# Linear attention with memories beside a mixture of experts: a tile's local sums called with its memories, and fixed preferences in the planner of TensorE's order

## The chip, the cores and the metric

The kernel runs on one core of one Trainium2 chip, in one launch. The metric is the time of an execution in microseconds on the device. All numbers are 32-bit floats.

## The reference

The kernel computes one layer over 4096 tokens (4 sequences of 1024) with 256 channels: `x + attention(xn) + ffn(xn)`, where `xn` is the normalized `x`. Cut to what matters:

```
q, k, v = split(xn @ w_q.T), split(xn @ w_k.T), split(xn @ w_v.T)   # 16 heads of 16 channels
sq, sk = elu(q) + 1, elu(k) + 1

# memories: a sum of four ("coarse") and each of the four ("fine"), mixed by a learned gate
a_c, n_c = sq @ M, sq @ z                  # M, z: sums over the 4 memories and their norms
out_coarse = a_c / clip(n_c)
out_fine = sum over m of softmax(mean n_f)[m] * (sq @ memory[m]) / clip(sq @ norm[m])
gprob = sigmoid(relu(out_coarse @ eg_w1.T + eg_b1) @ eg_w2.T + eg_b2)
memory_output = gprob * out_fine + (1 - gprob) * out_coarse

# local: causal linear attention in chunks of 128 tokens, with a state S, z carried along
scores = (sq_chunk @ sk_chunk.T) * mask
num = scores @ v_chunk + sq_chunk @ S      # local sums, and those of the state
den = scores.sum(-1) + sq_chunk @ z
S, z = S + sk_chunk.T @ v_chunk, z + sk_chunk.sum()

output = (gate * memory_output + (1 - gate) * num / clip(den)) @ w_o.T

# ffn: 8 experts of 176, two per token by a softmax, and a shared one of 352
y = sum over the 2 experts of weight * ((silu(xn @ wg.T) * (xn @ wu.T)) @ wd.T) + shared(xn)
```

## The kernel before

The 4096 tokens are 32 tiles of 128, in 8 blocks of 512. The kernel first loads, normalizes and turns the input and computes values and the experts' logits; then it sorts tokens into 71 tiles of 128 expert slots while the first projections and the first block of the shared expert run. After that come 34 rounds, one for each tile of attention with its tail, with the 71 expert tiles spread over rounds 2 to 29 and the shared expert and the projections beside them. At the end the experts' sums are read back from memory and added.

Attention of a tile `n` consists of short functions, each of which issues one engine's work. TensorE's are called units here:

- `scores(n)` (L746): 16 matmuls of 16 or 32 rows into `quad`, a PSUM tile of four banks, all heads' scores.
- `mask(n, g)` (VectorE, L753), four of them: `quad` times the causal mask into the buffers `sT`, of which there are four, one for each `g`.
- `memory(n)` (L889): 8 matmuls with 32 rows of queries as weights and 170 columns, into `quad` again. It needs all four masks, which read `quad` before it is overwritten.
- `weigh(n)`, `fine(n, c)` (VectorE) and `gate_coarse(n)`, `sum_fine(n)` (GpSimd): the weighted coarse and fine outputs from `quad`. The next `scores` need both `fine`.
- `local(n)` (L772): 16 matmuls of 32 columns of values as weights, with `sT`, into a bank `pn`. It too needs the four masks, and the masks of tile `n + 1` need it, since they write `sT`.
- `local_copy(n)` (ScalarE, L784), then `back(n)` (L793, L799): the local sums turned back, with the state's product added in the same bank `pb`; then `weigh_local`, `base` and `update`, `state`, `add_state`.
- `turned(n)` (L950), `gate_hidden(n)` (L976), `gate_sum`, `gate_out`, `blend`: the gate between coarse and fine, and the transposition for the output product; `output(n)` (L1071, L1075).

An expert tile `j` is `expert_turn` (L1166, waits for the gathered rows `xg`, L1133), `expert_hidden` (L1183), `expert_out` (L1215), and a scatter-add `put` (L1229).

The order on each engine is not written by hand. A list `order` gives each function a place; `plan(order)` then simulates the engines with a table `cost`, the needs of each function (`needs`), four rotating PSUM banks, and calls the functions in the order found. Each of TensorE's functions gets a due time, which is the sum of the costs before it in `order`. At each step the planner looks at the next call of each function that has all its needs, finds when it could begin, and takes for TensorE the one with the earliest beginning, and among equals the smallest due time:

```
limit = window + min(place of the next call of each of TensorE's functions)
...
begin = max(ready, free[engine])
rank = (begin, due if engine == "PE" else ready)
if engine not in best or rank < best[engine][0]:
    best[engine] = rank, f
```

Calls whose place lies beyond `limit` aren't considered; `window` is 12 (in the same planned microseconds). In the list of a round, `memory` and `weigh` come first, then `gate_hidden` of the tile before and `fine`, then `local`, then `back` and `update`.

## Time and profile before

| | before |
|---|---|
| median of 3 runs | 651.66 us (651.62 to 651.92) |
| the profiled execution | 651.07 us |
| its span | 649.4 us |
| granted clock of TensorE | 0.998 of full speed |
| TensorE's matmuls busy | 627.6 us |
| VectorE, GpSimd, ScalarE busy | 429.5, 408.6, 278.5 us |

A float matmul shows as two records in the trace, so the 16 matmuls of `local` are 32 rows, and the 8 of `memory` 16. Records of matmuls overlap, since the engine is pipelined and their ends are modelled; the distance between the starts of two successive units tells what the first one takes. Groups are named by the tile that they write and those that they read: `quad<-mem,sqT` is `memory`, `quad<-sqT,skT` and `quad<-sqT,skO` are `scores`, `pn<-sT,va` is `local`, `pb` is `back`, `pu<-va,sk` is `update`, `phe` is `expert_hidden`, `pye` is `expert_out`, `pte` is `expert_turn`, `ph` is `gate_hidden`.

### The profile page before, as it was taken

Reading aid. Unit: us, or ns where it says so; the run is one execution under the profiler, and the core shown is the slowest. Engines: PE = TensorE matmul, PEld = TensorE weight load, DVE = VectorE, ACT = ScalarE, POOL = GpSimd, SP = SyncE. Lnnn points to the kernel's source line nnn. Section 1 sums busy time; section 2 is a strip of 40 time slices with the busy share of each in tenths; the row PEclk is TensorE's granted clock in tenths of the full one; section 3 lists DMA queues with packets and bytes.
Section 4 is the critical chain, followed back from the end, with each engine's and each line's share of the span. In section 5 each row is a group of like instructions: output and inputs, shape, how many; then the busy total and the mean of one; then the engine's idle time right before and its main releaser. Section 6 shows DMA issues by size and latency. Waiting matters only on the chain.

```text
span 649.4 us, 15187 instructions
## 1 busy us (share of the span) xinstructions
PE 627.6 (97%) x5510; PEld 487.9 (75%) x5510; DVE 429.5 (66%) x1205; ACT 278.5 (43%) x676; POOL 408.6 (63%) x456
## 2 busy tenths in 40 slices
PE   4999999989999999999999999999999999999996
PEld 3884467778888877777786777788888886778775
DVE  6837999966665566566656765666655656667751
ACT  3765455444444454334533444333445434344320
POOL 5310055677777876565665665677777498586876
PEclk9999999999999999999999999999999999999999
DMA  9779000156566753443443444346666675564278
GB/s 301 242 238 248 0 1 2 50 168 166 133 152 144 164 129 87 106 107 77 109 118 78 106 107 98 89 106 138 154 151 160 149 161 127 147 164 99 26 225 301
DMA packets 94379, 86.51 MB, mean 133 GB/s; under 512 B 12033, under 2 KB 91905, under 8 KB 94177
## 3 DMA queue, kind: packets, MB, share of 16 engines
q1 hardware_dynamic: 78976, 65.34, 34.5%
q0 software_dynamic: 13632, 18.62, 16.6%
q10 hardware_dynamic: 1696, 1.58, 0.7%
q8 instruction: 44, 0.72, 0.5%
q14 instruction: 31, 0.25, 0.1%
HBM read 67.56 MB, written 23.59 MB: 140 GB/s over the span
## 4 chain that ended last, share of the span: by engine, by line
PE 89%; DVE 6%; ACT 1%; DMA 1%; issue 1%; POOL 0%; DVEq 0%
PE phe L1183 14%; PE pye L1215 11%; PE po L1071 6%; PE psu L1030 6%; PE pg L1010 5%; PE quad L746 5%; PE pn L772 5%; PE pv L407 5%; PE po L1075 4%; PE quad L889 4%; PE pq L649 3%; PE pk L649 3%; PE pte L1166 3%; PE pb L793 2%; PE pb L799 2%; PE found L617 2%
## 5 line engine op out<-in xcount | busy, mean ns | idle before, releaser
L1229 POOL DMA_INDIRECT sums<-y,islot x71 | 112.6, 1585 | 56.5 <-ACT y L1224 16.1
L1183 PEld LDWEIGHTS phe<-turned,wgu 128*128 128x128 f32 (+1 forms) x852 | 102.2, 187 | 14.9 <-issue 12.9
L1183 PE MATMUL phe<-turned,wgu 128*128 128x128 f32 (+1 forms) x852 | 108.0, 276 | 0.0
L1133 POOL DMA_INDIRECT xg<-xns,islot x71 | 71.4, 1006 | 58.0 <-PE pte L1166 43.9
L753 DVE TENSOR_TENSOR sT<-quad,causal 128x512 f32<-128x512 f32 x128 | 79.4, 682 | 21.9 <-PE quad L746 9.5
L1215 PE MATMUL pye<-wdn,hidden 112*128 112x256 f32 (+1 forms) x284 | 77.9, 396 | 0.5
L1200 DVE SCALAR_TENSOR_TENSOR the<-the,phe 128x256 f32<-128x256 f32 x71 | 29.5, 415 | 43.3 <-ACT the L1195 30.0
L1215 PEld LDWEIGHTS pye<-wdn,hidden 112*128 112x128 f32 (+1 forms) x284 | 48.8, 190 | 11.4 <-issue 3.2
L936 POOL TENSOR_TENSOR fm<-fm 128x512 f32<-128x512 f32 x32 | 48.2, 1506 | 4.2 <-DVE fm L923 4.2
L1224 ACT ACTIVATE y<-pye,wslot 128x256 f32<-128x256 f32 x71 | 33.4, 471 | 38.9 <-PE pye L1215 36.2
L1195 ACT ACTIVATE the<-phe 128x256 f32<-128x256 f32 x71 | 27.1, 382 | 51.6 <-PE phe L1183 45.8
L608 POOL TENSOR_TENSOR held<-ones,two 128x213 f32<-128x213 f32 (+1 forms) x22 | 16.3, 748 | 49.5 <-DVE ones L581 49.5
L1071 PE MATMUL po<-wd,h 128*128 128x256 f32 (+1 forms) x192 | 47.0, 380 | 0.0
L1010 PE MATMUL pg<-xnT,wg 128*128 128x512 f32 (+1 forms) x96 | 45.7, 598 | 0.5 <-DVE th L1040 0.5
L1030 PE MATMUL psu<-xnT,wu 128*128 128x512 f32 (+1 forms) x96 | 45.9, 600 | 0.0
L923 DVE TENSOR_TENSOR fm<-quad,rw 128x512 f32<-128x512 f32 x64 | 41.0, 682 | 0.2
L1071 PEld LDWEIGHTS po<-wd,h 128*128 128x128 f32 (+1 forms) x192 | 35.5, 190 | 6.1 <-issue 1.6
L916 POOL TENSOR_TENSOR cg<-coarse,gates 128x256 f32<-128x256 f32 x32 | 30.9, 964 | 13.9 <-DVE coarse L904 11.6
L1173 ACT COPY turned<-pte 128x256 f32<-128x256 f32 x71 | 26.5, 373 | 27.6 <-PE pte L1166 25.6
L1002 POOL TENSOR_TENSOR o<-o,loc 128x256 f32<-128x256 f32 x32 | 29.7, 929 | 7.8 <-ACT o L996 5.8
L772 PE MATMUL pn<-sT,va 128*32 128x128 f32 x1024 | 34.6, 276 | 0.0
L827 POOL TENSOR_TENSOR loc<-loc,cg 128x256 f32<-128x256 f32 x32 | 26.5, 827 | 12.7 <-DVE loc L817 12.0
(200 smaller groups left out, 1329.8 us busy)
## 6 DMA issues: line engine op xcount, KB each, us to landing
wdn<-in_w_down_dram SPq DMA_DIRECT2D x71, 224.0 KB
wgu<-in_w_gate_dram SPq DMA_DIRECT2D x71, 176.0 KB
wgu<-ups SPq DMA_DIRECT2D x71, 176.0 KB
xns<-x SPq DMA_DIRECT2D x8, 512.0 KB
sums<-in_x_dram SPq DMA_DIRECT2D x8, 512.0 KB
x<-in_x_dram SPq DMA_DIRECT2D x7, 512.0 KB
part<-sums SPq DMA_DIRECT2D x12, 256.0 KB
out_dram<-acc SPq DMA_DIRECT2D x12, 256.0 KB
```

The lines of the kernel that those rows point to most:

```text
L649: nc.tensor.matmul(pq, w[:, k, c * P : (c + 1) * P], xnT[:, k, :], start=(k == 0), stop=(k == NC - 1),)
L753: nc.vector.tensor_mul(sT, quad[:, g, :].rearrange("p (c t) -> p c t", t=P), causal[:, None, :].to_broadcast([P, NC * 2, P]),)
L772: nc.tensor.matmul(pn[CW * r : CW * (r + 1), q, :], wide[:, i, first : first + CW], st["sT", h // 2][:, c * 2 + h % 2, :], start=True, sto ...
L923: nc.vector.tensor_mul(fm[:, c].rearrange("p g m (r k) -> p g (m r) k", k=HD), quad[:, :, c * KM + KX + KN : (c + 1) * KM].rearrange("p g ...
L936: nc.gpsimd.tensor_add(fm[:, :, 0:2, :], fm[:, :, 0:2, :], fm[:, :, 2:4, :])
L1010: nc.tensor.matmul(pg[:n, :], wg[:, k, f * P : f * P + n], xnT[:, k, :], start=(k == 0), stop=(k == NC - 1),)
L1030: nc.tensor.matmul(pu[:n, :], wu[:, k, f * P : f * P + n], xnT[:, k, :], start=(k == 0), stop=(k == NC - 1),)
L1071: nc.tensor.matmul(po[:, :H], st["h", blk, f][:k, tok], wd[:k, f, :], start=(f == 0), stop=False)
L1133: nc.gpsimd.indirect_dma_start(out=xg, out_offset=None, in_=xns, in_offset=bass.IndirectOffsetOnAxis(ap=islot[:, j : j + 1], axis=0),)
L1183: nc.tensor.matmul(ph[: cols.stop - cols.start, s, :], wgu[:, k].rearrange("p g f -> p (g f)")[:, cols], xgT[:, k, :], start=(k == 0), sto ...
L1215: nc.tensor.matmul(py[:, :H], hT[:n, f, :], wdn[:n, f, :], start=(f == 0), stop=(f == 1))
L1229: nc.gpsimd.indirect_dma_start(out=sums, out_offset=bass.IndirectOffsetOnAxis(ap=islot[:, j : j + 1], axis=0), in_=st.pop(("y", j)), in_of ...
```

## The change

`memory(n)` now calls the matmuls of `local` (renamed `local_sums`) right behind its own, so they are one unit for the planner: its cost is 1.73 where `memory` had 0.85 and `local` 1.05, its needs are those of `memory` (the same four masks), it takes the bank that `local` took, and `local_copy` follows it. The entry of `local` in a round's list is gone, and `memory` has the weight of both. In `weigh` and `gate_coarse` the coarse output is kept under a second name, which changes no instruction.

The planner gets a table `prefer`: a fixed amount for each of TensorE's kinds of units is added to the due time when units that could begin at the same moment are compared. `window` goes from 12 to 14.

```diff
-    def local(n):
+    def local_sums(n):
...
+    def memory(n):
+
+        blk, i, tok = at(n)
+        sqT = st["sqT", blk]
+        for c in range(NC):
+            for g in range(NG):
+                rows = slice(32 * g, 32 * (g + 1))
+                nc.tensor.matmul(
+                    quad[:, g, c * KM : (c + 1) * KM], sqT[rows, c, tok], mem[rows, c, :],
+                    start=True, stop=True,
+                )
+        local_sums(n)
...
-        u += unit(560, memory, n) + unit(64, weigh, n)
+        u += unit(1120, memory, n) + unit(64, weigh, n)
 
         u += unit(256, gate_hidden, n - 1) + unit(64, fine, n, 0)
-        u += unit(560, local, n) + unit(64, fine, n, 1)
+        u += unit(64, fine, n, 1)
...
-            gate_hidden: [gate_sum], local: [local_copy], back: [weigh_local, base],
+            gate_hidden: [gate_sum], memory: [local_copy], back: [weigh_local, base],
...
-            scores: ("PE", 1.10), memory: ("PE", 0.85), local: ("PE", 1.05), back: ("PE", 0.92),
+            scores: ("PE", 1.10), memory: ("PE", 1.73), back: ("PE", 0.92),
...
-                mask: lambda: [(scores, n), (local, n - 1)],
+                mask: lambda: [(scores, n), (memory, n - 1)],
...
-                local: lambda: [(mask, n, g) for g in range(NG)],
-                local_copy: lambda: [(local, n), (back, n - 1)],
+                local_copy: lambda: [(memory, n), (back, n - 1)],
...
+        prefer = {
+            add_slots: -1.2, shared_gate: 1.4, scores: 4.0, shared_up: 4.2, keys_back: -1.1,
+            memory: -1.8, back: 2.9, update: 1.5, turned: -0.1, gate_hidden: -0.2, output: 3.6,
+            expert_turn: 1.7, expert_hidden: 1.9, expert_out: 0.5, project: -2.3,
+            batch_weights: 2.9,
+        }
         done, called = {}, {}
-        window = 12.0
+        window = 14.0
...
-                rank = (begin, due if engine == "PE" else ready)
+                rank = (begin, due + prefer.get(f, 0.0) if engine == "PE" else ready)
```

More of the change, by code (lines that the diff above doesn't have):

```diff
@@ L880, in add_state @@
         nc.gpsimd.tensor_add(new, new, old)
-    def memory(n):
-        blk, i, tok = at(n)
-        sqT = st["sqT", blk]
-        for c in range(NC):
-            for g in range(NG):
-                rows = slice(32 * g, 32 * (g + 1))
-                nc.tensor.matmul(
-                    quad[:, g, c * KM : (c + 1) * KM], sqT[rows, c, tok], mem[rows, c, :],
-                    start=True, stop=True,
-                )
     def weigh(n):
@@ L908, in weigh @@
             )
-        st["coarse", n] = coarse
+        st["coarse", n] = st["coarse to gate", n] = coarse
         st["rw", n] = rw
@@ L913, in gate_coarse @@
     def gate_coarse(n):
-        coarse = st["coarse", n]
+        coarse = st.pop(("coarse to gate", n))
         cg = tmp.tile([P, H], FP, tag="cg", name=f"cg_{n}", bufs=1)
```

## The prediction

> **What bounds the kernel now.** I read the page from the top, then the waits of TensorE, then TensorE's timeline unit by unit, because the page alone cannot say what a "busy" TensorE is busy with.

> ```profile
> span 649.4 us, 15187 instructions
> PE 627.6 (97%) x5510; PEld 487.9 (75%) x5510; DVE 429.5 (66%) x1205; ACT 278.5 (43%) x676; POOL 408.6 (63%) x456
> ...
> PE   4999999989999999999999999999999999999996
> ...
> DVE  6837999966665566566656765666655656667751
> ...
> PEclk9999999999999999999999999999999999999999
> ...
> PE 89%; DVE 6%; ACT 1%; DMA 1%; issue 1%; POOL 0%; DVEq 0%
> ```

> TensorE is busy in 97% of the span at full clock, and 89% of the chain that ended last is its own. Only slices 5 to 8 of the row DVE (65 to 115 us, where the expert lists are sorted and turned into slots) show another full engine. From there on the time is the length of TensorE's queue: what its units cost in their order, plus what it waits. The waits are short:

> ```profile
> PE pt L385 <- ACT x L367: 8.7, 2, 7.6
> PE pb L793 <- ACT nT L784: 2.4, 2, 1.2
> PE pte L1166 <- DMA xg<-xns,islot: 2.2, 2, 1.4
> PE pte L1166 <- issue: 1.1, 1, 1.1
> ```

> The first is the load of the input, which no edit touches. The second is two places where back (L793) stood waiting for local_copy (L784). The third is the first two gathers of expert rows.

> The timeline of TensorE shows what the busy share hides. A unit's price is the distance from its first start to the next unit's first start:

> ```profile
> 594.66 1.49 PE L1183 MATMUL phe<-turned,wgu 128*128 128x128 f32 x12
> 596.08 0.86 PE L889 MATMUL quad<-mem,sqT 32*128 32x170 f32 x16
> 596.88 1.13 PE L1215 MATMUL pye<-wdn,hidden 112*128 112x256 f32 x4
> 597.85 0.55 PE L976 MATMUL ph<-w,oc 128*128 128x64 f32 x4
> 598.24 1.55 PE L1183 MATMUL phe<-turned,wgu 128*128 128x128 f32 x12
> 599.71 1.08 PE L772 MATMUL pn<-sT,va 128*32 128x128 f32 x32
> 600.73 1.13 PE L1215 MATMUL pye<-wdn,hidden 112*128 112x256 f32 x4
> ...
> 608.53 0.86 PE L889 MATMUL quad<-mem,sqT 32*128 32x170 f32 x16
> 609.33 1.08 PE L772 MATMUL pn<-sT,va 128*32 128x128 f32 x32
> 610.34 0.73 PE L860 MATMUL pu<-va,sk 128*128 128x136 f32 x4
> ```

> The twelve records of phe last 1.42 us ahead of memory (594.66 to 596.08) and 1.47 ahead of local (598.24 to 599.71). Between two units of whole 128 x 128 weights the same twelve take 1.33 (the median of 44 units). So entering a unit of small weights costs 0.09 us, and into local up to 0.15. Leaving one costs too: pye behind memory takes 0.97 (596.88 to 597.85) where 0.87 is its price elsewhere. The last three lines are one of two places where this order already has local directly behind memory: memory still takes 0.80 and local 1.01, their prices everywhere. The step between them costs nothing, though one is 32 x 128 and the other 128 x 32.

> **The change part by part.**

> *Local behind memory.* It removes no instruction: the changed order has the same 623 units on TensorE with the same matmuls. It removes neighbours. Before, 30 of 32 tiles have other units between memory and local. Each pays four switches: into memory, out of it, into local, out of it. As one unit it pays the first and the last. Going through the order of before:
> - Entries into local that go, by the unit in front: 12 behind expert_out, 6 behind gate_hidden, 4 behind expert_hidden, 8 behind others. At 0.09 to 0.15, and 0.12 in the mean, 30 x 0.12 = 3.7 us.
> - Exits from memory that go: 15 into expert_out at 0.10, 6 into the short expert_turn at 0.055, 9 into others at 0.10: 2.8 us.

> Together 6.5 us. Scores keeps its own switches, which both orders have 32 times. Two or three tiles lie where VectorE is full, and there TensorE would only wait longer, so I count 28 of 30: **-5.9 us**.

> [...]

> *The wait for local_copy.* Before, back stands one expert_hidden behind local: 1.43 to 1.46 us of TensorE's work in half of the tiles. The copy alone is short, but ScalarE runs in order:

> ```profile
> 533.56 0.59 ACT L784 COPY nT<-pn 128x512 f32<-128x512 f32 x1 [3.23 <-PE pte L1166]
> ```

> ScalarE sat 3.23 us at an instruction ahead of this copy, waiting for expert rows to be turned, and back waited for both. In the changed order the median distance from local to back is 5.95 us and only two tiles are under 2. The row of 2.4 us goes. In the first rounds expert_turn 1 also moves behind back, which puts 0.9 us of work over its wait of 0.75 (what the row of 2.2 us has besides the first gather's 1.44). **-3.15 us**. The wait of 1.44 stays: the distance from the last slots to expert_turn 0 is the same in both orders. So does that of 1.1.

> *What the earlier call does to VectorE.* Masks of tile n+1 write the four buffers that local of tile n reads. In 6 tiles of before, local stands behind the next scores, and the masks show it:

> ```profile
> 205.87 2.48 DVE L753 TENSOR_TENSOR sT<-quad,causal 128x512 f32<-128x512 f32 x4 [2.10 <-PE pn L772]
> ```

> In the changed order local is at least 4.6 us ahead of the next scores, so this wait goes. It cost TensorE nothing before, as memory stood far behind. Weigh waits for memory's last matmul and not for local's: no cost. If it did wait 1.0 us more, the shortest way from memory to the next scores has 5.6 us, and weigh and both fines end 3.1 to 5.7 us behind memory, so nearly all of it would stay covered.

> *Preferred kinds and the wider window.* They trade distances. From the changed order, priced with the units above, against how long each chain took in the trace of before:
> - Scores to memory (four masks between): the median distance falls from 6.25 to 4.55 us, with 13 tiles at 2.99 to 3.92. The masks end 2.62 us behind the scores at best and 3.47 in the median, which includes the wait for local just shown. At 2.62 no tile waits; at 3.47 five do, for 1.45 us in all. I take the middle, 0.7.
> - Gate_hidden to turned (gate_sum, gate_out, blend on GpSimd): the median falls from 9.4 to 6.0, with seven tiles at 3.8 to 5.0. The chain took 2.99 at best and 5.05 in the median, with slack. At the median these seven would wait 4.3 us, at the best 0. I take 0.6, near the low end, since GpSimd's order is laid out anew for the nearer use.
> - Expert_hidden to expert_out: five at 2.45 and one at 1.76, against a median of 1.81: 0.1. At the ninth decile of 2.62 it is 1.7.
> - Turned to output and turned to gate_hidden grow (2.9 to 5.2, 6.6 to 9.5): nothing, and no gain, as TensorE did not wait there.

> Together **+1.4 us**, between 0 and 7.5. At the end, the last scatter on GpSimd moves forward, ahead of the gate of tile 30, so the parts are read back no later. The 12 totals (14.2 us) start right behind base of tile 31 and still end about with the last output; no cost. If they ended last, it would be by under 1 us. DMA traffic is the same.

> **Sum.** -5.9 - 3.15 + 1.4 = -7.65. The profiled span of 649.4 becomes 641.75. Its run took 651.07, so 1.67 lies around the span; the median of the runs shown, 651.66, is 0.6 above it. 641.75 + 1.67 + 0.6 = **644.0 us**.

> **The rivals.**

> [...]

> *Slower: the masks become TensorE's wait.* Memory, with local now behind it, stands nearer to its scores. If VectorE is behind its queue when the scores end (weigh_local and the silu of an expert stand just ahead of the masks), memory waits, and everything in TensorE's queue waits with it. Priced over the 32 distances: masks that end 4.25 us behind the scores in every tile cost 9.0 us, which eats both gains, and that is the point from which it decides. At 4.63 (the ninth decile before) they cost 15.1 us: 651.7 - 9.05 + 15.1 = 657.7. For it: VectorE at 66%, half of the tiles at or under 4.55. Against it: the long chains of before are mainly those that waited for local, and at the median chain the bill is 1.45.

> [...]

> **How the numbers follow.** The trace's own price of a switch with the short stalls: 0.65. The drain that stays: 0.22. Small waits that eat it, from no change to a little slower: 0.07. Masks that bind: 0.06. Two runs of this kernel can be told apart from about 0.2%, or 1.3 us. Faster by more takes the first two: 0.87. Of the third, 0.04 is within 0.2% and the rest is slower: 0.04 and 0.09. The range runs from 640.5 (no new waits, all 30 tiles, and something of the 1.44) to 649.5 (the drain that stays, with half of the small waits).

> **What would show it.** In the changed profile, phe ahead of memory should still take 1.42, memory 0.79 and local 1.01 with no gap between; phe, pye and the others should stand at their plain prices wherever local used to follow. The row of pb waiting for nT should be gone. [...] If masks bind, a row of quad waiting for sT on VectorE appears with several us. I am wrong if TensorE's busy time is not about 6 us below 627.6, or if its waits grow by more than they lose.

## The result: 3.2% slower, with the saved switches in it

The changed kernel takes 672.54 us (four runs, 670.84 to 673.82), that of before 651.64: a ratio of 1.0322, 95% interval 1.0295 to 1.0348. The profiled execution took 673.15 us, its span is 671.4. The forecast was 644.0.

The page after, in the lines that answer to those shown of before:

```profile
span 671.4 us, 15218 instructions
PE 632.0 (94%) x5510; PEld 494.9 (74%) x5510; DVE 437.6 (65%) x1205; ACT 280.2 (42%) x676; POOL 409.3 (61%) x456
...
PE   4999999999999889999998999999998999998996
...
PEclk9999999979999979999999999999999899998998
...
PE 74%; DVE 10%; POOL 10%; DMA 2%; ACT 2%; issue 2%; POOLq 0%; ACTq 0%
```

TensorE's share of the last chain fell from 89% to 74%, and GpSimd, which had none, now has 10%. The row PEclk has dips where before had full clock up to the last slice: the granted clock is 0.979 in the mean, where before had 0.998. TensorE's waits (total, times, longest):

```profile
PE pt L951 <- POOL o L1003: 9.4, 10, 2.2
...
PE pt L951 <- DVE hidden L1206: 3.7, 1, 3.7
PE pk L851 <- ACT y L1225: 3.4, 1, 3.4
PE pte L1167 <- DMA xg<-xns,islot: 2.4, 1, 2.4
PE pte L1167 <- issue: 2.1, 1, 2.1
```

The row of pb waiting for nT is gone, as foretold. In its place stands turned (`pt`) waiting for blend on GpSimd, ten times, and two single waits over 3 us.

TensorE's busy time, where about 6 us less was to be seen, is 4.4 us more (632.0 against 627.6): matmuls at half clock are busy too (from 138.40 to 141.80 us, at a granted 0.50, TensorE is busy all of the 3.40 us), so this sign can be read only in a run without them, further down.

The switches are gone too. All 32 tiles have memory directly in front of local, and there are 64 entries into units of small weights, where there were 94. The median distance from an expert_out to the next unit fell from 0.97 to 0.87 us, its price without a switch. TensorE's timeline at the first expert tiles:

```profile
131.00 0.86 PE L788 MATMUL quad<-mem,sqT 32*128 32x170 f32 x16
131.79 1.08 PE L772 MATMUL pn<-sT,va 128*32 128x128 f32 x32
132.80 0.66 PE L977 MATMUL ph<-w,oc 128*128 128x64 f32 x4
135.83 0.66 PE L1167 MATMUL pte<-ident,xg 128*128 128x128 f32 x2 [2.37 <-DMA xg<-xns,islot]
...
139.38 2.67 PE L1184 MATMUL phe<-turned,wgu 128*128 128x128 f32 x12
141.88 0.38 PE L1167 MATMUL pte<-ident,xg 128*128 128x128 f32 x2
```

Memory takes 0.79 us and local 1.01, with nothing between: over all 32 tiles 0.791 to 0.794 and 1.010 to 1.012. But phe, at 139.38, takes 2.50 us (to 141.88) for what costs 1.33 elsewhere. That is half clock (0.50 granted from 135.0 to 141.8), behind a wait of 2.37.

To see where the 22 us of span come from, I priced both orders of TensorE with the same plain prices and switches, and took the rest, unit by unit, as wait or half clock (units whose neighbours both are in the records). A wait is here all that lies above the price of the unit in front, a little more than the idle time in the profile's list (15.0 for turned, where the list has 9.4 and 3.7):

| us | before | after |
|---|---|---|
| the order at plain prices with its switches | 611.7 | 604.9 |
| above the price, in all | 16.4 | 44.0 |
| of it, ahead of 66 us | 4.1 | 4.1 |
| waits of turned | 0.3 | 15.0 |
| waits of expert_turn | 3.6 | 6.0 |
| waits of keys_back | 0.5 | 3.8 |
| waits of back | 3.2 | 0.3 |
| units at half clock, by its stretches in the middle | - | 9.1 |

The order got 6.8 us cheaper. The rest got 27.6 dearer, two thirds of it as waits and a third as half clock behind four waits of 2.23 to 3.69 us.

### The profile page after: what moved, and what is told of

The parts are those of the page before. It is cut to its first block, busy times and chain, and to the rows that moved or that the text cites. A ratio compares the mean times of both kernels' runs of the same rounds, so it can differ in the third digit from the quotient of the medians.

```text
span 671.4 us, 15218 instructions
## 1 busy us (share of the span) xinstructions
PE 632.0 (94%) x5510; PEld 494.9 (74%) x5510; DVE 437.6 (65%) x1205; ACT 280.2 (42%) x676; POOL 409.3 (61%) x456
## 3 DMA queue, kind: packets, MB, share of 16 engines
q0 software_dynamic: 13632, 18.62, 16.4%
## 4 chain that ended last, share of the span: by engine, by line
PE 74%; DVE 10%; POOL 10%; DMA 2%; ACT 2%; issue 2%; POOLq 0%; ACTq 0%
PE phe L1184 11%; PE pye L1216 7%; PE psu L1031 5%; PE quad L746 5%; PE po L1072 5%; PE pv L407 5%; PE pg L1011 4%; PE pn L772 4%; PE quad L788 4%; PE pq L649 3%; PE po L1076 3%; PE pk L649 3%; PE pt L951 2%; PE found L617 2%; POOL sums L1230 2%; PE pte L1167 2%
## 5 line engine op out<-in xcount | busy, mean ns | idle before, releaser
L1230 POOL DMA_INDIRECT sums<-y,islot x71 | 113.1, 1593 | 68.8 <-DMA sums<-y,islot 11.8
L1184 PE MATMUL phe<-turned,wgu 128*128 128x128 f32 (+1 forms) x852 | 113.4, 285 | 0.2 <-ACT sk L860 0.2
L1184 PEld LDWEIGHTS phe<-turned,wgu 128*128 128x128 f32 (+1 forms) x852 | 105.3, 194 | 6.7 <-issue 4.7
L753 DVE TENSOR_TENSOR sT<-quad,causal 128x512 f32<-128x512 f32 x128 | 79.4, 682 | 19.3 <-PE quad L746 16.7
L1216 PE MATMUL pye<-wdn,hidden 112*128 112x256 f32 (+1 forms) x284 | 75.3, 387 | 0.0
L1216 PEld LDWEIGHTS pye<-wdn,hidden 112*128 112x128 f32 (+1 forms) x284 | 50.3, 194 | 9.1 <-issue 3.9
L937 POOL TENSOR_TENSOR fm<-fm 128x512 f32<-128x512 f32 x32 | 46.8, 1462 | 6.7 <-DVE fm L924 6.7
L917 POOL TENSOR_TENSOR cg<-coarse,gates 128x256 f32<-128x256 f32 x32 | 25.6, 801 | 39.4 <-DVE coarse L905 39.1
L797 ACT COPY nT<-pn 128x512 f32<-128x512 f32 x32 | 18.7, 585 | 43.5 <-PE pn L772 43.5
L840 POOL TENSOR_TENSOR loc<-loc,cg 128x256 f32<-128x256 f32 x32 | 29.7, 930 | 10.8 <-DVE loc L830 10.7
L1003 POOL TENSOR_TENSOR o<-o,loc 128x256 f32<-128x256 f32 x32 | 31.1, 971 | 6.2 <-ACT o L997 5.0
```

The lines of the kernel that those rows point to most:

```text
L753: nc.vector.tensor_mul(sT, quad[:, g, :].rearrange("p (c t) -> p c t", t=P), causal[:, None, :].to_broadcast([P, NC * 2, P]),)
L937: nc.gpsimd.tensor_add(fm[:, :, 0:2, :], fm[:, :, 0:2, :], fm[:, :, 2:4, :])
L1184: nc.tensor.matmul(ph[: cols.stop - cols.start, s, :], wgu[:, k].rearrange("p g f -> p (g f)")[:, cols], xgT[:, k, :], start=(k == 0), sto ...
L1216: nc.tensor.matmul(py[:, :H], hT[:n, f, :], wdn[:n, f, :], start=(f == 0), stop=(f == 1))
L1230: nc.gpsimd.indirect_dma_start(out=sums, out_offset=bass.IndirectOffsetOnAxis(ap=islot[:, j : j + 1], axis=0), in_=st.pop(("y", j)), in_of ...
```

## The experiments

Each kernel's ratio is against before on its own chip and in the same rounds. "Charged" means that the planner counts something; "in the same order" means that only what a call issues differs.

**The merge alone, and the preferences alone.** The kernel after with `window` at 12 calls everything in the same order, so the window counts for nothing. The merge alone has no `prefer`:

```diff
-                rank = (begin, due + prefer.get(f, 0.0) if engine == "PE" else ready)
+                rank = (begin, due if engine == "PE" else ready)
```

> The merge without the table of preferences (the window is 12; with 14 the planner's order is the same). Theory: the switches saved (64 entries into small-weight units instead of 94, 6.6 us by the prices of the trace of before) were real, and the lost time came with the preferences, which cut the distances to blend and to the banks. Then this kernel has TensorE's waits of before or fewer, no half-clock stretches in the middle, and 643 to 648 us. Rival: the merge itself ties units together and makes the waits; then 660 to 675 us.

Measured: 663.17 us, ratio 1.0192 (1.0143 to 1.0242). The theory failed. The merge without any preference already makes three fifths of the whole loss. It has the cheap order (605.1, 64 entries) and pays for it with waits, and with three stretches of half clock in the middle, 13.7 us in all (the changed kernel has four, 23.9 us; at 2.50 us for a phe of 1.33, a little under half of such a stretch is lost at most):

```profile
PE pt L951 <- POOL o L1003: 4.5, 3, 2.3
PE pte L1167 <- DMA xg<-xns,islot: 2.6, 1, 2.6
PE pte L1167 <- DVE loc L830: 2.2, 1, 2.2
PE po L1072 <- DVE skT L673: 2.1, 1, 2.1
```

The preferences alone put `prefer` and the window of 14 into the kernel before.

> The table of preferences and the window of 14 on the kernel before, with memory and local separate units (local has no preference). Theory (preferences make the waits): TensorE waits 10 us or more beyond before, for blend and for banks, with half-clock stretches: 660 to 672 us. Rival (only the merged unit with preferences does harm): 648 to 655 us, as 3 entries fewer are worth under 1 us.

Measured: 662.37 us, ratio 1.0186 (1.015 to 1.0221), as the theory had it. TensorE waited for blend in six places, and two stretches of 3.4 us ran at half clock:

```profile
PE pt L950 <- POOL o L1002: 8.9, 6, 2.5
```

So each half of the change makes waits on its own, and together they come to somewhat less than their sum (1.9% and 1.9%, and 3.2% for both).

**Whose fault the waits are: the same order with a cause left out.** Three of the longest waits stand behind batch_weights. These are VectorE, GpSimd and TensorE there (start, duration; the wait in front in brackets):

```profile
231.53 2.52 DVE L711 TENSOR_TENSOR rel<-rel,top 128x64 f32<-128x64 f32 x1
...
232.16 1.81 POOL L937 TENSOR_TENSOR fm<-fm 128x512 f32<-128x512 f32 x1
...
235.51 0.41 DVE L1201 SCALAR_TENSOR_TENSOR the<-the,phe 128x256 f32<-128x256 f32 x1
235.95 0.29 DVE L1203 SCALAR_TENSOR_TENSOR hidden<-the,phe 112x128 f32<-112x128 f32 x1
236.25 0.29 DVE L1206 SCALAR_TENSOR_TENSOR hidden<-the,phe 64x128 f32<-64x128 f32 x1
...
236.69 0.66 PE L951 MATMUL pt<-ident,o 128*128 128x128 f32 x2 [3.69 <-DVE hidden L1206]
```

Turned waits for the last instruction of an expert's silu. It doesn't use its result: it needs the PSUM bank that this instruction frees, and silu stood behind the softmax in VectorE's queue. The planner counts batch_weights as one TensorE unit of 3.50 us, and nothing on VectorE. It does so in the order of before too. But the softmax itself grew: from its first VectorE instruction to its last it took 6.5 us here and 6.1 in the sequence at 515 us, where those of before took 2.6 to 3.0. The excess lies in a few instructions beside GpSimd's; the longest here, the product L711 with 2.52 us, ends at 234.05, just behind GpSimd's fm (233.97). In the next kernel the last three sequences leave the softmax out:

```diff
+        if b:
+            st["w5", b] = st["w5", 0]
+            return
         top = small.tile([P, NC, HC], FP, tag="top", name=f"top_{b}", bufs=1)
```

> The changed kernel in the same order on every engine, but the softmax over memories is done for the first of four sequences alone and its weights used for all (leaves out 10 VectorE and 1 ScalarE instructions for each of three sequences; the matmul of batch_weights and one copy stay). Theory: three of the longest waits (3.9, 3.5 and 2.3 us, at 233, 516 and 355 us) follow these blocks, because VectorE and so the release of PSUM banks is late by them, and two of them set off stretches at half clock (10.2 and 3.4 us, 6.8 us lost). They go: 655 to 660 us. Rival: these waits have another cause and stay: 668 to 673 us.

Measured: 657.19 us, ratio 1.0098 (1.0073 to 1.0123): as expected. The three waits and both stretches of half clock behind them are gone, and the waits of turned for blend stay:

```profile
PE pt L954 <- POOL o L1006: 13.1, 11, 3.0
```

The two other stretches are gone in this execution as well, though the first gather still holds TensorE 2.1 us, and there is a new one at 528.6, behind the wait of 3.0. So the gain of 15 us is mainly the softmax's, and in part a matter of where the half clock fell.

The waits of turned for blend are GpSimd's queue. Here is one of them, in GpSimd's rows and TensorE's:

```profile
606.34 1.59 POOL L1230 DMA_INDIRECT sums<-y,islot  x1 [1.16 <-DMA sums<-y,islot]
...
607.38 1.30 POOL L1003 TENSOR_TENSOR o<-o,loc 128x256 f32<-128x256 f32 x1
608.06 1.34 POOL L893 TENSOR_TENSOR state<-state,state 128x272 f32<-128x272 f32 x1
...
608.74 0.44 PE L951 MATMUL pt<-ident,o 128*128 128x128 f32 x2 [2.23 <-POOL o L1003]
...
609.23 2.58 PE L1184 MATMUL phe<-turned,wgu 128*128 128x128 f32 x12
```

Blend (L1003) stands behind a put that first waits 1.16 us for the put before it to land and then takes 1.59, to 607.93. GpSimd's records overlap, as TensorE's do: blend's begins before the put's ends, and ends at 608.68, 0.75 us behind it. That is blend's usual 0.73; its 1.30 are no slower addition. Then turned starts, and the phe behind it runs at half clock. In the next kernel put issues nothing:

```diff
     def put(j):
-        nc.gpsimd.indirect_dma_start(...)
+        st.pop(("y", j))
```

> The changed kernel in the same order, with the scatter-add of the experts' rows left out on GpSimd (71 instructions; the output lacks the experts). Theory: the waits of turned for blend (9.4 us in ten places, one followed by a half-clock stretch at 609 us) come from blend standing behind a put in GpSimd's queue, which itself waits for the expert's output or for the put before to land. They go: 656 to 662 us, and the page shows no row of pt waiting for o on GpSimd. Rival: blend is late through ScalarE's or VectorE's part of its chain: within 3 us of the changed kernel.

Measured: 649.61 us, ratio 0.9997 (0.9982 to 1.0011). Turned's waits fell from 15.0 to 1.3 us, none for blend on GpSimd. From the start of gate_hidden to the end of blend the median fell from 5.53 to 3.70 us. The gain, 23 us, is larger than expected, since the two long waits behind the softmax are shorter as well (keys_back 1.3 us where it had 3.5, turned 1.3 where it had 3.9), and half clock costs 4.0 instead of 9.1 us (three stretches of 3.4 us). The softmax took 3.9 us in these two places instead of 6.5 and 6.1, so the two causes touch each other.

Both left out:

> The changed kernel in the same order, with both left out: the scatter-add of the experts' rows on GpSimd, and the softmax over memories of the last three sequences. Theory: the two causes account for nearly all of the new waits, so what is left is the saved switches: no row of pt waiting for o, none of pk or pte waiting for ScalarE, at most the half-clock stretch at the first gather, and 639 to 644 us (about 8 under the run without put, which still had 6 us of waits behind the softmax and 3 us of half clock after them). Rival: waits move to other places once these are gone: 647 us or more.

Measured: 642.65 us, ratio 0.9866 (0.9837 to 0.9895), as expected. Its waits:

```profile
PE pt L385 <- ACT x L367: 8.9, 2, 7.7
PE pte L1170 <- DMA xg<-xns,islot: 1.8, 1, 1.8
PE found L617 <- ACT held L598: 1.5, 2, 0.9
PE quad L791 <- DVE sT L756: 0.5, 1, 0.5
```

This is the forecast's time in the changed order, without half clock in the middle. TensorE's busy time is 619.4 us, 8.2 below before, and it is done at 633.0 us instead of 644.0. Leaving the two out takes away the whole loss, and more. They aren't separate sums: left out one by one they give 15 and 23 us, together 30. And before itself was not run with the two left out, so what it would gain, and how near the forecast this comes by chance, stays open. It is no version of the kernel: the output lacks the experts and uses one sequence's weights for all.

**Can it be mended with everything computed?** The softmax as a call of its own for the planner:

```diff
-            update: ("PE", 0.48), ..., batch_weights: ("PE", 3.50),
+            update: ("PE", 0.48), ..., batch_weights: ("PE", 0.36), batch_softmax: ("DVE", 2.9),
```

> The changed kernel with the softmax of batch_weights made a call of its own for the planner (VectorE, 2.9 us, after a TensorE unit of 0.36; before it was one TensorE unit of 3.50), and weigh made to need it. All is computed. Theory: the planner then knows that VectorE is taken and leaves the waits behind batch_weights out, as leaving out the softmax did (657 us): 655 to 663 us. Rival: the lateness comes from GpSimd and VectorE contending, which no charge mends: 668 to 674 us.

Measured: 658.65 us, ratio 1.0114 (1.0082 to 1.0146): as expected. Charging the work brought nearly as much as leaving it out, though the planner's order changes with it. The softmaxes still took 3.8 to 4.8 us beside GpSimd's work, so the rival's cause may be there too, but a charge did mend most of the loss. In the profiled execution (655.16 us, the fastest of four) no half clock is left in the middle.

Then I asked the planner for more distance, in general: longer delays from each engine's end to its consumers and a dearer put, with preferences and without.

```diff
-        lag = {"PE": 0.22, "ACT": 0.06, "DVE": 0.06, "POOL": 0.06, "SP": 4.0}
+        lag = {"PE": 0.22, "ACT": 0.40, "DVE": 0.40, "POOL": 1.50, "SP": 4.0}
```

> The changed kernel with the softmax charged as its own call, a put counted as 2.2 us and 3.5 to land, and the planner's delay from an engine's end to its consumers raised (GpSimd 0.06 to 1.5, VectorE and ScalarE 0.06 to 0.4 us). The order then keeps gate_hidden to turned at 8.0 us in the median instead of 6.0, with the same 64 entries. Theory (switches saved, waits avoidable): most waits of turned go, no half clock in the middle: 642 to 650 us, faster than before. Rival (the merged order cannot have cover for all): 653 us or more.

> The merge without preferences, with the softmax charged, the put counted as above, and wider delays (GpSimd 3.0, VectorE and ScalarE 0.8 us). Gate_hidden to turned becomes 8.0 us in the median (6.7 with the merge alone), one at 3.5. Theory: 643 to 652 us, against 663 for the merge alone. Rival: 655 us or more.

Measured: 666.39 us, ratio 1.0216 (1.0189 to 1.0244), and 665.02, ratio 1.0209 (1.0179 to 1.0238). Both missed. In the first, turned's waits fell to 6.1 us, but others came (expert_turn 4.8, expert_hidden 2.9, output 2.4), and the end moved to another chain. The last expert_out began at 608.3 us and the last put only at 635.0. So the experts' sums were read back late, the totals on GpSimd ended at 659.7, and TensorE, done at 652.9, was 13 us ahead of the end. Before, its last put began at 617.8 and it was 5.4 ahead. A delay that the planner believes in also moves the puts back.

A put that stands back for whatever can begin within 1.5 us, again with the softmax charged, and with a gather's landing counted as 3.6 us instead of 2.0, so this is more than one change:

```diff
+        late_by = {put: 1.5}
...
-                rank = (begin, due + prefer.get(f, 0.0) if engine == "PE" else ready)
+                rank = (begin + late_by.get(f, 0.0), due + prefer.get(f, 0.0) ...)
```

> The changed kernel with the softmax charged as its own call, a gather counted as 3.6 us to land, and one rule more for GpSimd's queue: a put stands back for anything that can begin within 1.5 us of it in the plan. Theory (blend late behind a waiting put): turned waits 3 us or less for o, 647 to 654 us, against 658.7 with the softmax charged alone. Rival (the planner uses the earlier blend to pull turned forward again, and the waits stay): 656 to 662 us.

Measured: 702.87 us, ratio 1.0714 (1.066 to 1.0769), the worst of all. Turned's waits were 4.8 us, but the puts fell behind: the last expert_out began at 634.7 us, the last put at 669.4. Expert outputs waited in their three buffers, and TensorE waited for ScalarE, which writes them and frees their banks:

```profile
PE po L1077 <- DVE acc L1089: 6.4, 1, 6.4
PE pye L1221 <- ACT y L1230: 5.2, 3, 3.6
PE phe L1189 <- ACT y L1230: 4.3, 3, 2.5
PE pb L811 <- DVE hidden L1211: 2.9, 4, 1.7
PE pb L811 <- ACT y L1230: 2.8, 1, 2.8
```

**The order of before, with local moved and nothing else.** The planner works with before's costs and its own place for local; memory issues local's matmuls:

```diff
     def local(n):
+        pass
...
+        local_sums(n)        # at the end of memory(n)
```

> The order of before, planned with its own costs and no preferences; only the 16 matmuls of local are called right behind memory's, where the planner had them some units later. All 590 other units of TensorE stand in the same order as before (and so the cover that before's plan gave to every chain, less the 0.2 us a tile of saved switches). Theory (the switches are worth 6.5 us where the cover stays; what was lost is the planner's repacking around a bigger unit): 64 entries, no half clock in the middle, 643 to 647 us. Rival A (holding the bank of local's sums longer makes other units wait for a bank): 650 to 656 us. Rival B (the merge can't be had without the waits): over 656 us.

Measured: 662.88 us, ratio 1.0109 (1.0062 to 1.0156). Before took 655.84 us in these rounds. The theory failed again. By its size this is rival B's case (over 656 us), while rival A, with 650 to 656, names a good part of the waits:

```profile
PE pb L795 <- ACT nT L786: 4.8, 8, 1.0
PE ph L979 <- DVE sqT L669: 2.1, 4, 0.5
PE ph L979 <- DVE skT L673: 2.1, 4, 0.5
PE pte L1169 <- DVE ph L990: 2.1, 1, 2.1
PE pye L1218 <- ACT oc L968: 1.8, 4, 0.5
```

Gate_hidden (`ph`) has no use for sqT or skT, nor expert_out (`pye`) for oc. They wait for the banks that these instructions free. As I read it, local's sums now hold a bank for some units longer, while local_copy keeps its place in ScalarE's queue, and with four banks in rotation the next units find none. Back's waits for local_copy grew as well, from two to eight. And the one long wait, 2.1 us of the first expert_turn, was followed by 6.8 us at half clock.

**GpSimd out of the chain to turned.** One VectorE instruction in place of ScalarE's product and GpSimd's addition, in the order of the kernel with the softmax charged:

```diff
-        nc.scalar.activation(o, st.pop(("diff", n)), AF.Copy, scale=prob)
-        nc.gpsimd.tensor_add(o, o, st.pop(("base", n)))
+        nc.vector.scalar_tensor_tensor(
+            o, st.pop(("diff", n)), st.pop(("prob", n)), st.pop(("base", n)), ALU.mult, ALU.add
+        )
```

> The changed kernel with the softmax charged as its own call (658.7 us), in the same order of calls, but blend is one VectorE instruction (diff times prob plus base, about 0.42 us) in place of a ScalarE product (0.51) and a GpSimd addition (0.73 to 1.3). No put stands ahead of it any more. Theory: the waits of turned (7 us in eight places for o on GpSimd) go: 644 to 652 us, with everything computed. Rival (VectorE, in order too, makes turned wait as long): 656 us or more.

Measured: 654.06 us, ratio 1.0019 (0.9997 to 1.0042). The row of turned waiting for GpSimd is gone, and as with the softmax charged there is no half clock in the middle of the profiled execution (649.58 us, the fastest of ten); turned's waits fell from 9.8 to 3.5 us, now for VectorE's queue and for banks. It is the time of before, not less: the forecast of 644 to 652 was missed by 2 us. TensorE's busy time shows the saved switches here, with everything computed:

```profile
PE 621.4 (96%) x5510; PEld 485.7 (75%) x5510; DVE 454.1 (70%) x1237; ACT 265.6 (41%) x644; POOL 388.6 (60%) x424
```

That is 6.2 us below before's 627.6, and with the softmax charged alone it is 5.1 below. The time doesn't follow: the idle time between TensorE's records adds up to 20.7 us, and to 16.4 before.

> The kernel before in its own order, with the same blend on VectorE. Theory: before has 9 us of cover for this chain in the median and no wait of turned, so nothing is gained: within 2 us of before, or slower by VectorE's additional 13 us of work spread over the span. Rival (the move helps any order): 3 us or more faster than before.

Measured: 649.81 us, ratio 0.9985 (0.9956 to 1.0014): no difference that can be told, as expected. The median of before was 652.99 in these rounds, but its runs lie between 648.82 and 654.81.

> As j2, but the planner is told (blend 0.45 on VectorE, gate_out 0.50 on ScalarE) and packs turned nearer again: gate_hidden to turned 5.5 us in the median, many at 3.8. Theory (the planner spends any cover that it sees): slower than j2 by 3 us or more. Rival: the same as j2 or faster.

Measured: 657.43 us, ratio 1.0069 (1.0028 to 1.0111). Told of the faster blend, the planner spent the cover at once, and it cost 3.4 us.

> The merge alone (663 us) in its order of calls, with blend on VectorE. Its waits for o on GpSimd were 4.5 us in three places, two of them ahead of a half-clock stretch (540 and 595 us, 10 us at half). Theory: 652 to 657 us. Rival: banks and the first gather (eturn 5.8, output 3.7 us) bind it alone: 660 us or more.

Measured: 657.52 us, ratio 1.0079 (1.0046 to 1.0112), against 1.0192 for the merge alone, half a microsecond beyond what the theory said.

No version that computes everything beat the kernel before beyond doubt. The nearest is before itself with blend on VectorE.

## Why the prediction was wrong

*Local behind memory, -5.9 us.* Right, and the size too. The order is 6.8 us cheaper at the prices of the trace, and where no half clock falls in the middle TensorE's busy time is 5.1 to 6.2 us lower with everything computed. (Small slips in the working change nothing: 30 x 0.12 is 3.6 and the exits come to 2.7, so it is 28 of 30 of 6.3 that makes 5.9; and slices 5 to 8 end at 130 us, not 115.) A drain of TensorE between memory and local, which the range's poor end and a chance of 0.22 count, is shown by no run: the two places of before became 32, and memory (32 x 128) takes 0.791 to 0.794 us with local (128 x 32) right behind it, where it took 0.791 to 0.793 before, with other units behind 30 of the 32.

*The wait for local_copy, -3.15.* Mostly right. Back's waits fell from 3.2 to 0.3 us, and expert_turn 1's wait of 0.75 is gone. But the wait of expert_turn 0, which I took to stay at 1.44, grew to 2.37, and what follows it runs at half clock. The same gather took 5.67 us from its issue to TensorE's start where it had 4.72; why isn't shown.

*Preferred kinds and the wider window, +1.4, between 0 and 7.5.* This step failed: the waits that the shorter distances would make. It isn't the preferences' alone, since the merge without them shortens the same distances (gate_hidden to turned to 6.7 us in the median) and loses 12 us. Term by term:
- Masks, 0.7: no wait of quad for sT is in the list of TensorE's waits. The rival that was to end slower had the wrong mechanism.
- Gate_hidden to turned, 0.6, with 4.3 as the poor end: 15.0 measured, a quarter of it the one wait for a bank. I set the changed distances against the chain's shortest and median times of before, and took a value near the shortest, "since GpSimd's order is laid out anew". The new order did not shorten the chain: puts that wait for the put before are in GpSimd's queue in either order (8.9 us of such waits before, 11.8 in the changed kernel). And the median of before was not slack. It was what this queue takes: from the start of gate_hidden to the end of blend the median is 5.28 us before, 5.53 in the changed kernel, and 3.70 without the puts.
- Banks: not in the sum at all. I followed each chain from producer to consumer, and never asked which instruction frees the bank that a unit takes. The waits of keys_back (3.8) and that of turned behind the softmax (3.9) are of this kind. The moved-only kernel, where waits for banks come to more than the saving, shows that this would have needed its own place in the sum.
- Half clock: not in the sum. 9.1 us, in four stretches, behind waits of 2.37, 3.69, 3.35 and 2.23 us.

*The bound on the poor side.* The range ended at 649.5, since I took the waits as independent and each at most as long as the chain of before at its median. They were not: behind four waits of 2.2 to 3.7 us the clock was halved, which adds to what the wait itself costs, and a put or a softmax that is late makes several units wait.

The sum was also made about the wrong thing. "From there on the time is the length of TensorE's queue" holds for the order of before, whose list of waits is short. It isn't a property of the kernel: the same cheap queue gave 642.65 us with two bodies of work left out, and 672.54 with them.

## What to carry to other kernels

TensorE at 97% was bound by its own queue only as long as the order kept its cover (651.64 us, and 672.54 with the cheaper queue); before pricing a shorter queue, list for every unit what it waits for, *including who frees its buffer*, and compare with the time that chain took in its queue, not with its shortest. A planner that packs against optimistic costs can turn a saving into less cover, as it did here when told of a faster blend; work that it doesn't charge (here a softmax booked on another engine) shows up as waits somewhere else, of units that don't use its result. To find the cause, keep the order fixed and leave one body of work out: three such kernels named the two causes and what they cost together, where none of the changes of the planner gave an order faster than before's. The same cut in the kernel before belongs beside them, and is missing here.

## What the runs showed of the hardware

```profile
131.60:135.00 3.40, 1.86 (x44) 1.00 0.86 234
135.00:138.40 3.40, 2.57 (x12) 0.50 0.33 80
138.40:141.80 3.40, 3.40 (x18) 0.50 0.18 52
230.60:234.00 3.40, 1.55 (x7) 1.00 0.44 54
234.00:237.40 3.40, 0.71 (x4) 0.50 0.62 162
237.40:240.80 3.40, 3.40 (x39) 0.50 0.10 24
240.80:244.20 3.40, 3.40 (x17) 0.50 0.42 58
356.85:360.26 3.41, 1.88 (x14) 1.00 0.62 173
```

The four stretches at half clock begin at 135.0, 234.0, 520.7 and 609.4 us, which are 29, 113 and 139 times 3.41 us apart from the first, and last 6.83, 10.24, 3.41 and 3.41 us, one to three times the same 3.41. So the changes of the clock fall on a beat of 3.41 us in this run. It isn't tied to the kernel's start: with the merge alone the first stretch begins at 135.8, 0.8 us later on the beat. The first stretch ended behind one full window of work (138.40), the second behind two (237.40 and 240.80). Counted on the beat itself, the windows ahead of the four drops hold 1.89, 1.59, 1.09 and 1.19 us of work, so none of them was idle, and the clock fell to 0.50; behind the window with 1.88 us, in the last line, which has a wait of 2.08, it stayed at 1.00. So busy time alone, with the modelled ends of matmuls in it, does not draw the line. Nor does the length of the wait: waits of 2.23 and 2.37 us had a drop behind them, the one of 2.08 had none, and one of 2.1 in the moved-only kernel had.

A VectorE product of 128 x 64 elements took 2.52 us beside GpSimd's work where its like took 0.23 elsewhere. It is one of six instructions of the softmax, in the two long places, that took 0.64 to 3.22 us where the same ones take 0.17 to 0.23 in the short places, all beside GpSimd's. The changed order isn't the only one: with the merge alone two of the softmaxes take 5.1 and 5.7 us, and without puts 3.9. That the two engines hold each other up was not tried by itself.
